# A four-image vision-mixer, attention and expert layer: one TensorE product beside each round of the last attention loop, gathers of the first three images moved into that loop, and 34 of 48 products delta*u moved from the first stage into the loops

## The chip, the cores and the metric

The kernel runs on one core of a Trainium2 chip. The metric is the device time of that core in microseconds (us), the median of three runs.

## The reference

The input is four images of 64 x 64 tokens with 128 channels. Layer 0 adds a scan mixer to them: a group norm, a projection to 256 inner channels and a gate, and then, in three orders of the tokens (forward, backward, sliced), a causal convolution of four taps, SiLU, the projections to delta, B and C, and a selective scan with 16 states; a gate and an output projection follow. Layer 1 adds attention (16 heads of 8, a softmax over all 4096 tokens of an image), a small feed-forward, and last an expert layer in which each of 64 experts picks its 8 best tokens of each image:

```python
def step(h, inp):
    u_, de_, b_, c_ = inp
    dA = jnp.exp(de_[..., None] * A)
    h = h * dA + (de_ * u_)[..., None] * b_[:, None, :]
    y = jnp.einsum('bdn,bn->bd', h, c_)
    return (h, y)
...
delta = jax.nn.softplus(jnp.einsum('dr,brl->bdl', dt_w, dt_raw) + dt_b[None, :, None])
y = selective_scan(x, delta, A, Bm, Cm)
...
logits = jnp.einsum('bsd,ed->bse', x, gate_w) + gate_b
probs = jax.nn.softmax(logits, axis=1)
vals, idx = jax.lax.top_k(probs.transpose(0, 2, 1), K)
...
pooled = jnp.einsum('bked,bke->bed', gathered, topv)
h = jax.nn.gelu(jnp.einsum('ebd,edh->ebh', h, weight1), approximate=False)
out = jnp.einsum('ebh,eho->ebo', h, weight2)
```

Here `de_ * u_` is the product delta*u of the change, and `pooled` is what the gathers make.

## The kernel before

The kernel writes the order of instructions of every engine out by hand: pieces of work are Python generators, each `yield` of which ends a *step*, and a `Pace` (L1350) takes so many steps of a chain of generators whenever its `run` is called. What a step issues goes to the engines' queues in that order, and each engine works through its own queue in order. A generator yields the mark `PE` ahead of a step that issues a TensorE product, and `WAIT` where something that it needs is not made yet. `Bank` (L114) counts PSUM banks: `take` yields `PE`, and again while none is free.

The work is staged as follows (times of the profiled execution).

1. *Fill*, 0 to 2257 us (L1393 to L1399). `Inputs.of_chunk` (L334) makes the scan inputs of 48 chunks (four images, three orders, four chunks of 1024 tokens by 256 channels): convolution L364, SiLU L371, the projections L378 to L400, softplus (L404 to L427, its result `r` is delta). Its end stores delta, multiplies `u` by delta (L431, VectorE) and stores the product as `du` (L432); the stores go by `keep` (L346) to the POOL queue, 1 MB each. Meanwhile `Scans.of_image` (L461) runs the scans of image 0. An image has 384 scan steps; each loads delta and `du` again from memory (SP queue), makes the exponentials (L507, ScalarE), multiplies by B (L514), scans (L523), multiplies by C (L528, all VectorE), and sums over the states on TensorE (L534).
2. *Opening* of image 0, up to 2513 us: queries and values of the attention.
3. *Loops* of images 0 to 2: 2513 to 5066, 5068 to 7657 and 7659 to 10237 us. `Attention.loop` (L850) has 1024 rounds an image. A round of the loop issues four score products (L881, 32 rows of the array each, into two PSUM tiles of a pool of three), two exponentials of 128 x 1024 (L886, ScalarE), and four value products (L895) into an accumulator; it issues the scores of the following round ahead of its own values. After each round `beside(i)` is called. In these loops it runs the next image's scans, `after` of the image before, and the opening of the next one. All of them share one PSUM bank.
4. *Last loop* (image 3), 10240 to 12679 us (L1450 to L1459). Its blocks of 512 tokens are finished one after the other (`by_block`). `beside` is `last.run(0.8)`: four steps in five rounds of one chain, which holds the rest of `after` of image 2, the searches and choices of tokens of images 0 to 2, and `after` of image 3 for the blocks that are finished, all but the last block.
5. *Tail*, 12679 to 12991 us: `after` of the last block, in between the gathers of images 0 to 2 (`gathers.run(3.0)`), the choice of image 3, its gather, and the experts (`answers`, L1282), whose weights are loaded in rooms of 2 MB ahead of use (`prefetch`, L1276), and the scatter.

`Attention.after` (L938) makes for each block: the sums of the softmax loaded, their reciprocals, a store and a load of these, spread out (`shares`, L960); the context times the share (L982, `cT`), the product with `w_comb` (L989, `co`: two banks of two products), a residual and a norm (`first`, L971); cosines of eight columns (L1076, ScalarE); and in `second` (L1002) a transpose (`zT`, L1010), the feed-forward (four `h` products L1023 of 512 columns, then for each of four groups of tokens four `fo` products L1033), a norm, a transpose to `xT` (L1054) and the gate's logits (L1063, `lg`). Each of `co`, `zt`, `fo` and `xT` issues all products of a bank in one step: two, four, four, four. `Experts.search` (L1135) finds the eight best logits of each expert, `choice` (L1156) makes the tokens' weights, and `pool` (L1189), called by `gather` (L1219) once for each 512 tokens, makes `wt` (L1198, four products with a diagonal, one step) and `pool` (L1209, four, one step).

Of the kernel before, what the change touches and what calls it, by code (L numbers as in the profile page):

```python
# [113 lines left out]
class Bank:  # L114


    def __init__(self, pool, n):
        self.pool, self.free = pool, n
# [6 lines left out]
    def take(self, name):  # L125
        yield PE
        while not self.free:
            yield PE
        return self.grab(name)
# [5 lines left out]
def scan_weights(nc, const, load, load_ps, ident, in_proj_w, out_proj_w, dirs):  # L135
# [64 lines left out]
    return w_z, w_out, ws  # L200


class Inputs:
# [130 lines left out]
    def of_chunk(self, b, order, c):  # L334
# [96 lines left out]
        nc.vector.tensor_mul(u, r, u)  # L431
        keep("du", u)  # L432
# [4 lines left out]
class Scans:  # L437
# [23 lines left out]
    def of_image(self, b, made, alone=False):  # L461
# [54 lines left out]
        def step(s):  # L516

            order, c, k, j = steps[s]
            at = 4 * k + j
            dA, dB = tiles.pop(("delta", s)), tiles["du", s]  # L520
            h = self.deep.tile([P, T], F32, tag="h", bufs=2, name=f"h_{b}_{s}")
            first = 0.0 if c == 0 else ends[order, c - 1][:, at : at + 1]
            nc.vector.tensor_tensor_scan(h, dA, dB, first, ALU.mult, ALU.add)  # L523
            if c < NC - 1:
                nc.gpsimd.tensor_copy(ends[order, c][:, at : at + 1], h[:, T - 1 :])  # L525
            if s + 1 < n:
                inputs(s + 1)
            nc.vector.tensor_mul(dB, h, spread[order, c, "C", j % 2])  # L528

# [104 lines left out]
class Attention:  # L634
# [3 lines left out]
    def __init__(self, tc, ctx, w, gate, cols, ident, bank, dram, t1, w_out, sums, sz, x):  # L638
# [64 lines left out]
        self.xn, self.logits, self.angled, self.whole, self.closed = {}, {}, {}, {}, {}  # L703

# [27 lines left out]
    def tokens(self, b, g, angles):  # L732
# [48 lines left out]
        yield  # L781

# [155 lines left out]
    def after(self, b, gs=range(L // QB), to=None):  # L938
# [32 lines left out]
        def first(g):  # L971
# [13 lines left out]
            for half in range(2):  # L985
                ps = yield from self.bank.take(f"co_{b}_{g}_{half}")
                for k in range(2):
                    at = slice((2 * half + k) * P, (2 * half + k + 1) * P)
                    nc.tensor.matmul(ps[:, k * C : (k + 1) * C], cT[:, at], self.w_comb, start=True, stop=True)  # L989
                yield  # L990
                u_h = flat(u[:, 2 * half : 2 * half + 2, :])
                nc.vector.tensor_add(u_h, u_h, ps[:, : 2 * C])
                self.bank.leave()
# [8 lines left out]
        def second(g):  # L1002
# [6 lines left out]
            for k in range(4):  # L1009
                nc.tensor.transpose(ps[:D, k * P : (k + 1) * P], z[:, g * 4 + k, :], self.ident)  # L1010
            yield
# [9 lines left out]
            for f in range(4):  # L1021
                ps = yield from self.bank.take(f"h_{b}_{g}_{f}")
                nc.tensor.matmul(ps, self.w1[:, f * P : (f + 1) * P], zT, start=True, stop=True)  # L1023
# [6 lines left out]
            for k in range(4):  # L1030
                ps = yield from self.bank.take(f"fo_{b}_{g}_{k}")
                for f in range(4):
                    nc.tensor.matmul(  # L1033
                        ps[:, :C], h[:, f, k * P : (k + 1) * P], self.w2[:, f, :], start=(f == 0), stop=(f == 3)
                    )
                yield
# [16 lines left out]
            for k in range(4):  # L1053
                nc.tensor.transpose(ps[:, k * P : (k + 1) * P], u[:, k, :], self.ident)  # L1054
            yield
# [7 lines left out]
            nc.tensor.matmul(ps[rows], self.gate, xT, start=True, stop=True)  # L1063
# [31 lines left out]
class Experts:  # L1095
# [93 lines left out]
    def pool(self, b, g):  # L1189
# [6 lines left out]
        for i in range(4):  # L1196
# [4 lines left out]
            )  # L1201
        yield
# [5 lines left out]
        for i in range(4):  # L1208
            nc.tensor.matmul(ps[:, :E], x[:, i, :], wT[:, i, :], start=(i == 0), stop=(i == 3))  # L1209
        yield  # L1210
# [157 lines left out]
def tile_kernel(tc, ctx, x, in_proj_w, dirs, out_proj_w, attn, gate, weight1, weight2, out):  # L1368
# [45 lines left out]
    block.begin(loop)  # L1414
    with tc.manual_schedule():
# [34 lines left out]
    with tc.manual_schedule():  # L1450
        last = Pace(
            last.parts, experts.biases(),
            *(part for images in pairs[:-1] for part in (experts.search(images, blocks), experts.choice(images, blocks))),
# [3 lines left out]
        block.loop(nb - 1, lambda i: last.run(0.8), True)  # L1457
        last.rest()
    loop.close()  # L1459
    with ExitStack() as end:  # L1460
        block.bank = Bank(end.enter_context(tc.tile_pool(name="end_ps", bufs=7, space=PSUM)), 7)
        with tc.manual_schedule():
            room = experts.room(end, 3)
            gathers = Pace(experts.gather(range(nb - 1)))
            with ExitStack() as pieces:
                block.pieces_of(pieces, 1, opening=False)
                closing = block.after(nb - 1, range(blocks - 1, blocks), experts.rest(pairs[-1], blocks - 1))
                for i, _ in enumerate(closing):
                    if i == 2:
                        experts.prefetch(room, nc.scalar)  # L1470
                    gathers.run(3.0)
            for _ in experts.choice(pairs[-1], blocks - 1):
                gathers.run(3.0)
            gathers.rest()
            experts.prefetch(experts.room(end, 1), nc.scalar)
# [36 lines left out]
```

## Time and profile before

| What | Value |
|---|---|
| Runs | 12969.35, 12983.24, 12982.96 us (median 12982.96) |
| Profiled execution | 12992.53 us, span 12990.6 us |
| Mean TensorE clock granted | 0.958 |
| Fill, opening | 2257 us, 256 us |
| Loops of images 0, 1, 2 | 2553, 2589, 2578 us |
| Last loop | 2438 us |
| Tail | 312 us |

Busy times in the profile: PE is TensorE's products, PEld its weight loads, DVE VectorE, ACT ScalarE, POOL GpSimd, SP the SyncE queue, which only issues transfers. A busy time is a sum over stages of different kinds, so the views by stretch of time, which give the same columns for each stage, are read beside it. The lengths of TensorE's products are modelled; differences between starts are safer. The chain of waits follows the work back from the last instruction, at each step to what released it.

### The profile page before, as it was taken

How to read it: one execution, taken by the hardware profiler on the slowest of the kernel's cores; microseconds unless marked ns; L12 is line 12 of the kernel's file. 1: busy time of each engine (PE TensorE's matmuls, PEld its weight loads, DVE VectorE, ACT ScalarE, POOL GpSimd, SP SyncE). 2: the span in 40 equal slices, each digit the busy share in tenths (PEclk: the TensorE clock that was granted, in tenths of full speed). 3: DMA queues.
4: the chain of work that ended last, by engine and by line, in shares of the span. 5: the costliest groups of instructions: out<-in, count | busy, mean ns of one | idle time of the engine just before them, and what ended most of it. 6: DMA issues, size and time to landing. Idle time of an engine off the chain costs nothing.

```text
span 12990.6 us, 213981 instructions
## 1 busy us (share of the span) xinstructions
PE 12191.8 (94%) x85447; PEld 3937.0 (30%) x85447; DVE 8718.2 (67%) x8674; ACT 10713.3 (82%) x10808; POOL 2930.0 (23%) x3817
## 2 busy tenths in 40 slices
PE   7788888399999999999999999999999999999996
PEld 3333333122222222333322223333222223322225
DVE  6999999788888777888887778888874211121112
ACT  5676766399999988999999889999998888888881
POOL 3323232221212212223232123232321000000000
PEclk9898988699999999999999999999999999999996
DMA  5666776555444455444444445444443100000005
GB/s 157 195 202 195 208 199 190 159 124 122 119 122 111 111 132 134 125 117 111 115 110 110 130 132 126 117 110 116 112 110 97 51 19 11 18 24 11 16 14 183
DMA packets 688512, 1481.86 MB, mean 114 GB/s; under 512 B 187694, under 2 KB 304998, under 8 KB 687254
## 3 DMA queue, kind: packets, MB, share of 16 engines
q1 hardware_dynamic: 499294, 1055.63, 31.8%
q0 software_dynamic: 140192, 302.80, 7.6%
q10 hardware_dynamic: 48024, 109.74, 3.3%
q8 instruction: 669, 10.96, 0.4%
q14 instruction: 333, 2.73, 0.1%
HBM read 1158.77 MB, written 308.81 MB: 113 GB/s over the span
## 4 chain that ended last, share of the span: by engine, by line
PE 81%; DVE 7%; ACT 5%; issue 4%; DMA 3%; SPq 0%; POOL 0%; ACTq 0%; DVEq 0%; POOLq 0%
PE s L881 36%; PE acc L895 30%; PE y L534 4%; PE cv L364 3%; DVE h L523 3%; PE sp L422 2%; PE fo L1033 1%; ACT e L886 1%; PE h L1023 1%; PE xd L378 1%; DVE dB L514 1%; ACT ln L415 0%; DVE du L514 0%; PE out L761 0%; DVE r L427 0%
## 5 line engine op out<-in xcount | busy, mean ns | idle before, releaser
L886 ACT ACTIVATE e<-s 128x1024 f32<-128x1024 f32 x8192 | 7904.8, 1027 | 1053.5 <-PE s L881 882.8
L881 PE MATMUL s<-qm,qT 32*128 32x512 f32 x32768 | 5444.3, 642 | 120.8 <-ACT e L886 61.5
L895 PE MATMUL acc<-e,v 128*32 128x512 f32 x32768 | 4387.5, 607 | 23.8 <-ACT av L904 21.3
L881 PEld LDWEIGHTS s<-qm,qT 32*128 32x128 f32 x32768 | 1801.7, 184 | 3239.3 <-issue 1429.4
L525 POOL COPY ends<-h 128x1 f32<-128x1 f32 x1152 | 1275.0, 1108 | 3352.1 <-DVE h L523 3322.4
L895 PEld LDWEIGHTS acc<-e,v 128*32 128x32 f32 x32768 | 649.0, 108 | 3160.9 <-issue 3021.8
L523 DVE TENSOR_TENSOR_SCAN h<-delta,ends,du 128x1024 f32<-128x1024 f32 x576 | 1350.9, 2345 | 216.2 <-ACT delta L507 185.5
L523 DVE TENSOR_TENSOR_SCAN h<-dA,ends,dB 128x1024 f32<-128x1024 f32 x576 | 1350.6, 2345 | 149.2 <-ACT dA L507 145.8
L514 DVE TENSOR_TENSOR dB<-du,B 128x1024 f32<-128x1024 f32 x768 | 927.9, 1208 | 626.8 <-PE y L534 603.6
L507 ACT ACTIVATE delta<-delta,A 128x1024 f32<-128x1024 f32 x768 | 887.0, 1155 | 153.4 <-PE y L534 142.7
L507 ACT ACTIVATE dA<-delta,A 128x1024 f32<-128x1024 f32 x768 | 888.4, 1157 | 140.9 <-DMA delta<-d_delta 105.4
L528 DVE TENSOR_TENSOR du<-h,C 128x1024 f32<-128x1024 f32 x768 | 935.3, 1218 | 0.1
L528 DVE TENSOR_TENSOR dB<-h,C 128x1024 f32<-128x1024 f32 x768 | 935.0, 1217 | 0.0
L514 DVE TENSOR_TENSOR du<-du,B 128x1024 f32<-128x1024 f32 x768 | 920.9, 1199 | 0.0
L364 PE MATMUL cv<-xn,conv 128*128 128x512 f32 x1024 | 499.9, 642 | 25.7 <-DVE xn L299 17.3
L563 POOL DMA_DIRECT2D d_y<-o x512 | 327.6, 668 | 781.9 <-DVE o L550 720.3
L910 POOL DMA_DIRECT2D d_ctx<-av x512 | 263.4, 523 | 1055.8 <-ACT av L904 1046.5
L534 PE MATMUL y<-du,sel 128*32 128x256 f32 x6144 | 488.2, 391 | 13.1 <-DVE du L528 13.1
L534 PE MATMUL y<-dB,sel 128*32 128x256 f32 x6144 | 491.7, 393 | 3.4 <-DVE dB L528 3.4
L523 DVE TENSOR_TENSOR_SCAN h<-delta,du 128x1024 f32<-128x1024 f32 x192 | 438.4, 2283 | 52.0 <-ACT delta L507 45.5
L523 DVE TENSOR_TENSOR_SCAN h<-dA,dB 128x1024 f32<-128x1024 f32 x192 | 438.4, 2283 | 40.0 <-ACT dA L507 38.4
L1026 DVE TENSOR_SCALAR h<-h,b 128x512 f32<-128x512 f32 x124 | 92.7, 748 | 514.0 <-PE s L881 514.0
(256 smaller groups left out, 7648.6 us busy)
## 6 DMA issues: line engine op xcount, KB each, us to landing
delta<-d_delta SPq DMA_DIRECT2D x768, 512.0 KB
du<-d_du SPq DMA_DIRECT2D x576, 512.0 KB
du<-d_du ACTq DMA_DIRECT2D x192, 512.0 KB
d_u<-u POOLq DMA_DIRECT2D x48, 1024.0 KB, 5.8
B<-d_bc SPq DMA_DIRECT2D x96, 512.0 KB
C<-d_bc SPq DMA_DIRECT2D x96, 512.0 KB
d_delta<-r POOLq DMA_DIRECT2D x48, 1024.0 KB, 5.1
d_du<-u POOLq DMA_DIRECT2D x48, 1024.0 KB, 6.9
```

The costliest lines, as they stand in the source:

```text
L364: nc.tensor.matmul(ps[:, cut], w["conv"][:, k, m * P : (m + 1) * P], reads(k, g), start=(k == 0), stop=(k == 3))
L507: nc.scalar.activation(tiles["delta", s], t, AF.Exp, scale=A)
L514: nc.vector.tensor_mul(tiles["du", s], du, spread[order, c, "B", j % 2])
L523: nc.vector.tensor_tensor_scan(h, dA, dB, first, ALU.mult, ALU.add)
L525: nc.gpsimd.tensor_copy(ends[order, c][:, at : at + 1], h[:, T - 1 :])
L528: nc.vector.tensor_mul(dB, h, spread[order, c, "C", j % 2])
L534: nc.tensor.matmul(y[32 * g : 32 * g + 32, : T // 4], self.sel[:, j // 2, :], hC[:, 256 * g : 256 * g + 256], start=(j == 0), stop=(j == 3),)
L563: nc.gpsimd.dma_start(out=to.rearrange("p (i j) -> p i j", i=SLICES)[:, :, at : at + n], in_=rows.rearrange("p (i j) -> p i j", i=SLICES),)
L881: nc.tensor.matmul(s_ps[:, k, :], qT[at : at + 32, kc * P : (kc + 1) * P], queries[j, qb][at : at + 32, :], start=True, stop=True,)
L886: nc.scalar.activation(e, s_ps, AF.Exp, scale=1.0 / math.sqrt(D))
L895: nc.tensor.matmul(accs[j, qb][32 * k : 32 * k + 32, :], v[:, kc, h * VW : h * VW + 32], es[i][k // 2][:, k % 2, :], start=(kc == 0), stop ...
L910: nc.gpsimd.dma_start(out=self.context[b][h * D : h * D + D, cut], in_=av[32 * k : 32 * k + D, :])
```

## The change

- `Bank` gets a flag `patient`. While it is set and no bank is free, `take` yields `WAIT` and not `PE`.
- `early` names 14 chunks, the twelve of image 0 and two of image 1, that keep the product delta*u in the fill. For the other 34, `Scans.product(s)` makes it at the end of scan steps in loops 0 to 2 (not in the fill): eight pieces of 128 x 256 a chunk, for the chunk that comes next. In one step it loads 128 KB each of delta and u on the SP queue, two steps later it multiplies them (VectorE) and stores 128 KB to `d_du` on the POOL queue; the tiles have one buffer each. That is 272 pieces in all.
- `between` yields `PE` between the products of a bank while `fine` is set, which it is in the last loop only: `co`, `zt`, `fo` and `xT` then issue one product a step; `wt` and `pool` issue two.
- `h` and `lg`, one product of 512 columns each before, are two of 256 columns everywhere, in two steps in the last loop.
- The last loop's `beside` takes up to three steps of the chain that do not begin with a product, and then at most one that does.
- The gathers of images 0 to 2 stand in that chain, each behind its choice. In the tail, only image 3 is gathered, and the fourth room of weights is asked for ahead of the choice.

```diff
--- before.py
+++ after.py
@@ -115,7 +115,7 @@
 
 
     def __init__(self, pool, n):
-        self.pool, self.free = pool, n
+        self.pool, self.free, self.patient = pool, n, False
 
     def grab(self, name):
         assert self.free
@@ -125,6 +125,8 @@
     def take(self, name):
         yield PE
         while not self.free:
+            while self.patient and not self.free:
+                yield WAIT
             yield PE
         return self.grab(name)
 
@@ -200,6 +202,11 @@
     return w_z, w_out, ws
 
 
+def early(b, order, c):
+
+    return b == 0 or (b == 1 and order == 0 and c < 2)
+
+
 class Inputs:
 
 
@@ -428,8 +435,9 @@
             self.leave()
         self.middle = False
         keep("delta", r)
-        nc.vector.tensor_mul(u, r, u)
-        keep("du", u)
+        if early(b, order, c):
+            nc.vector.tensor_mul(u, r, u)
+            keep("du", u)
         self.made[b, order, c] = made
         yield
 
@@ -526,6 +534,27 @@
             if s + 1 < n:
                 inputs(s + 1)
             nc.vector.tensor_mul(dB, h, spread[order, c, "C", j % 2])
+            if not alone:
+                product(s)
+
+        def product(s):
+
+            order, c, k, j = steps[s]
+            part, turn = divmod(4 * k + j - 8, 3)
+            chunk = (b, order, c + 1) if c + 1 < NC else (b, order + 1, 0) if order < 2 else (b + 1, 0, 0)
+            if part < 0 or turn == 1 or chunk not in made or early(*chunk):
+                return
+            of, m, at = made[chunk], part // 4, part % 4 * (T // 4)
+            cut = slice(m * P, (m + 1) * P), slice(at, at + T // 4)
+            if turn == 0:
+                for name in ("delta", "u"):
+                    t = self.extra.tile([P, T // 4], F32, tag=f"x_{name}", name=f"x_{name}_{b}_{s}")
+                    nc.sync.dma_start(out=t, in_=of[name][cut])
+                    tiles["x", name] = t
+            else:
+                t, u = tiles.pop(("x", "delta")), tiles.pop(("x", "u"))
+                nc.vector.tensor_mul(t, t, u)
+                nc.gpsimd.dma_start(out=of["du"][cut], in_=t)
 
         def total(s, y):
             order, c, k, j = steps[s]
@@ -701,6 +730,7 @@
         self.small = ctx.enter_context(tc.tile_pool(name="a_small", bufs=2))
         self.u, self.q, self.v, self.context, self.total, self.t2 = {}, {}, {}, {}, {}, {}
         self.xn, self.logits, self.angled, self.whole, self.closed = {}, {}, {}, {}, {}
+        self.fine = False
 
     def begin(self, loop):
 
@@ -779,6 +809,11 @@
         turned(nc, a, turns.rearrange("p h d -> p (h d)"))
         self.angled[b] += 1
         yield
+
+    def between(self, k, n=4):
+
+        if self.fine and k + 1 < n:
+            yield PE
 
     def norm(self, out, src, name):
 
@@ -987,6 +1022,7 @@
                 for k in range(2):
                     at = slice((2 * half + k) * P, (2 * half + k + 1) * P)
                     nc.tensor.matmul(ps[:, k * C : (k + 1) * C], cT[:, at], self.w_comb, start=True, stop=True)
+                    yield from self.between(k, 2)
                 yield
                 u_h = flat(u[:, 2 * half : 2 * half + 2, :])
                 nc.vector.tensor_add(u_h, u_h, ps[:, : 2 * C])
@@ -1008,6 +1044,7 @@
             ps = yield from self.bank.take(f"zt_{b}_{g}")
             for k in range(4):
                 nc.tensor.transpose(ps[:D, k * P : (k + 1) * P], z[:, g * 4 + k, :], self.ident)
+                yield from self.between(k)
             yield
             zT = self.piece([D, 512], "p0", name=f"zT_{b}_{g}")
             nc.vector.tensor_scalar_mul(zT, ps[:D], self.cos_ry[:, 2:3])
@@ -1020,7 +1057,10 @@
             h = self.one.tile([P, 4, 512], F32, tag="h", bufs=max(1, self.n - 1), name=f"h_{b}_{g}")
             for f in range(4):
                 ps = yield from self.bank.take(f"h_{b}_{g}_{f}")
-                nc.tensor.matmul(ps, self.w1[:, f * P : (f + 1) * P], zT, start=True, stop=True)
+                for k in range(2):
+                    at = slice(k * 256, k * 256 + 256)
+                    nc.tensor.matmul(ps[:, at], self.w1[:, f * P : (f + 1) * P], zT[:, at], start=True, stop=True)
+                    yield from self.between(k, 2)
                 yield
                 if self.n == 2:
                     nc.vector.tensor_scalar(h[:, f, :], ps, self.b1[:, f : f + 1], 0.0, ALU.add, ALU.max)
@@ -1033,6 +1073,7 @@
                     nc.tensor.matmul(
                         ps[:, :C], h[:, f, k * P : (k + 1) * P], self.w2[:, f, :], start=(f == 0), stop=(f == 3)
                     )
+                    yield from self.between(f)
                 yield
                 nc.vector.tensor_add(u[:, k, :], u[:, k, :], ps[:, :C])
                 self.bank.leave()
@@ -1052,6 +1093,7 @@
             ps = yield from self.bank.take(f"xT_{b}_{g}")
             for k in range(4):
                 nc.tensor.transpose(ps[:, k * P : (k + 1) * P], u[:, k, :], self.ident)
+                yield from self.between(k)
             yield
             xT = self.piece([P, 512], "p0", name=f"xT_{b}_{g}")
             nc.vector.tensor_copy(xT, ps)
@@ -1060,7 +1102,10 @@
             yield
             ps = yield from self.bank.take(f"lg_{b}_{g}")
             rows = slice(E, 2 * E) if to else slice(0, E)
-            nc.tensor.matmul(ps[rows], self.gate, xT, start=True, stop=True)
+            for k in range(2):
+                at = slice(k * 256, k * 256 + 256)
+                nc.tensor.matmul(ps[rows, at], self.gate, xT[:, at], start=True, stop=True)
+                yield from self.between(k, 2)
             yield
             if to:
                 for t in to:
@@ -1199,6 +1244,7 @@
                 ps[:, i * E : (i + 1) * E], self.chosen[b // 2][rows, at : at + P], self.diagonal[rows, b // 2, :],
                 start=True, stop=True,
             )
+            yield from self.block.between(i, 3 if i == 1 else 0)
         yield
         wT = self.some.tile([P, 4, E], F32, tag="wT", name=f"wT_{b}_{g}")
         nc.vector.tensor_copy(wT.rearrange("p i e -> p (i e)"), ps[:, : 4 * E])
@@ -1207,6 +1253,7 @@
         ps = yield from bank.take(f"pool_{b}_{g}")
         for i in range(4):
             nc.tensor.matmul(ps[:, :E], x[:, i, :], wT[:, i, :], start=(i == 0), stop=(i == 3))
+            yield from self.block.between(i, 3 if i == 1 else 0)
         yield
         into = self.pooled[:, :, b]
         if g == 0:
@@ -1412,6 +1459,7 @@
     block.bank = bank
     loop = ExitStack()
     block.begin(loop)
+    scans.extra = loop.enter_context(tc.tile_pool(name="s_extra", bufs=1))
     with tc.manual_schedule():
         last = Pace()
         n = 3 * NC * NB
@@ -1450,29 +1498,40 @@
     with tc.manual_schedule():
         last = Pace(
             last.parts, experts.biases(),
-            *(part for images in pairs[:-1] for part in (experts.search(images, blocks), experts.choice(images, blocks))),
+            *(
+                part for images in pairs[:-1]
+                for part in (experts.search(images, blocks), experts.choice(images, blocks), experts.gather(images))
+            ),
             block.after(nb - 1, range(0, 4)), block.after(nb - 1, range(4, 6)), block.after(nb - 1, range(6, blocks - 1)),
             experts.search(pairs[-1], blocks - 1),
         )
-        block.loop(nb - 1, lambda i: last.run(0.8), True)
+        block.fine = bank.patient = True
+
+        def beside(i):
+
+            for _ in range(3):
+                if last.then is not PE:
+                    last.run(1.0)
+            if last.then is PE:
+                last.run(1.0)
+
+        block.loop(nb - 1, beside, True)
         last.rest()
+        block.fine = False
     loop.close()
     with ExitStack() as end:
         block.bank = Bank(end.enter_context(tc.tile_pool(name="end_ps", bufs=7, space=PSUM)), 7)
         with tc.manual_schedule():
             room = experts.room(end, 3)
-            gathers = Pace(experts.gather(range(nb - 1)))
             with ExitStack() as pieces:
                 block.pieces_of(pieces, 1, opening=False)
                 closing = block.after(nb - 1, range(blocks - 1, blocks), experts.rest(pairs[-1], blocks - 1))
                 for i, _ in enumerate(closing):
                     if i == 2:
                         experts.prefetch(room, nc.scalar)
-                    gathers.run(3.0)
+            experts.prefetch(experts.room(end, 1), nc.scalar)
             for _ in experts.choice(pairs[-1], blocks - 1):
-                gathers.run(3.0)
-            gathers.rest()
-            experts.prefetch(experts.room(end, 1), nc.scalar)
+                pass
             for _ in experts.gather(pairs[-1]):
                 pass
             for _ in experts.answers(end, out):
```

## The prediction, on record before the changed kernel ran

> **What bounds the kernel now.** I read the page first, then the fill, the loops and the tail each by themselves, because the page is an average over stages with different limits. On the page, TensorE is busy for 94% of the span and owns the chain that ended last. Its two attention lines (the scores of L881 and the values of L895) hold two thirds of that chain.
>
> ```profile
> PE 12191.8 (94%) x85447; PEld 3937.0 (30%) x85447; DVE 8718.2 (67%) x8674; ACT 10713.3 (82%) x10808; POOL 2930.0 (23%) x3817
> ...
> PE 81%; DVE 7%; ACT 5%; issue 4%; DMA 3%; SPq 0%; POOL 0%; ACTq 0%; DVEq 0%; POOLq 0%
> ```
>
> The busy times by stage (columns: stretch, length, then PE, PEld, DVE, ACT and POOL busy, PE clock, DMA share, GB/s) tell the stages apart: the fill, the first loop, the last loop, the tail.
>
> ```profile
> 0.00:2257.00 2257.00, 1875.71 (x6821) 755.29 (x6821) 2033.90 (x1543) 1526.08 (x1223) 730.28 (x909) 0.89 0.67 193
> 2513.00:5066.00 2553.00, 2538.18 (x19802) 733.75 (x19798) 2064.74 (x1673) 2387.75 (x2498) 591.44 (x809) 1.00 0.49 120
> 10240.00:12678.00 2438.00, 2415.54 (x17248) 708.98 (x17244) 368.36 (x947) 2016.18 (x2109) 178.81 (x313) 0.99 0.07 20
> 12678.00:12990.00 312.00, 214.80 (x1538) 170.63 (x1534) 89.15 (x201) 31.85 (x51) 26.05 (x47) 0.63 0.56 190
> ```
>
> The fill is nearest to VectorE (90%), both loops are TensorE's, and the tail is a chain of dependent steps with TensorE at 0.63 of its clock. The fill's groups give the product that the change moves 110 us of VectorE:
>
> ```profile
> L431 DVE TENSOR_TENSOR u<-r,u 128x2048 f32<-128x2048 f32 x48 | 110.0, 2292 | 1.7
> ```
>
> But the chain of waits in the fill alternates: for long stretches it runs between TensorE and ScalarE, and VectorE's work lies beside it (start, length, line).
>
> ```profile
> 1045.16 10.52 PE cv L364 x24
> ...
> 1055.70 1.12 ACT u L371
> ...
> 1056.87 2.84 PE xd L378 x6
> ```
>
> In the last loop I timed rounds by what stands beside them. In the timeline (start, length, line; lengths are modelled, so I take differences of starts):
>
> ```profile
> 10704.85 1.14 PE L881 MATMUL s<-qm,qT 32*128 32x512 f32 x8
> 10705.92 1.07 PE L895 MATMUL acc<-e,v 128*32 128x512 f32 x8
> 10706.92 1.37 PE L881 MATMUL s<-qm,qT 32*128 32x512 f32 x8
> 10708.22 1.07 PE L895 MATMUL acc<-e,v 128*32 128x512 f32 x8
> ...
> 11007.08 1.16 PE L1033 MATMUL fo<-w,h 128*128 128x128 f32 x8
> 11008.17 1.14 PE L881 MATMUL s<-qm,qT 32*128 32x512 f32 x8
> ...
> 11495.01 0.71 PE L989 MATMUL co<-w_comb,cT 128*128 128x128 f32 x4
> 11495.65 1.14 PE L881 MATMUL s<-qm,qT 32*128 32x512 f32 x8
> ```
>
> An empty round takes 2.07 us (10704.85 to 10706.92) or 2.30 (the next; its second scores wait 0.23 for the exponentials, there being three buffers), alternating. A burst of four fo products (eight passes) costs 1.09, two co products (four passes) 0.64. Of the co burst 0.21 pass before its second pass and 0.20 between its last pass and the next scores; the middle passes cost 0.11. So a product alone (two passes) costs about 0.21 + 0.20 = 0.42, against 0.27 as a quarter of the fo burst. In the tail, the gathers of images 0 to 2 stand between the closing's products, and the answers (L1240) start behind the last gather (chain of waits: start, length, line):
>
> ```profile
> 12751.49 2.00 PE fo L1033 x8
> 12753.49 1.60 PE pool L1209 x8
> 12755.09 1.90 PE wt L1198 x8
> 12756.99 2.00 PE fo L1033 x8
> ...
> 12857.62 1.97 PE pool L1209 x8
> 12859.99 1.97 PE h L1240 x8
> ```
>
> [...] 0.20 is lost where a 128-row product gives way to 32-row scores, and the co at 10265.21 held the attention for 2.2 us while its input came. [...] in the start of the last loop the reciprocal's store leaves at 10258.50 and the load behind it at 10260.85, landing at 10264.4.
>
> **Part 1, the fill.** 34 of 48 products leave: 34 x 2.29 = 78 us of VectorE and 34 stores on POOL. Following the chain over 0 to 2257, 17 of the 48 lie on it; of the moved ones that is 12 to 14. Where a product leaves that is not on the chain, the next wait (the convolution, L364, then ScalarE's L371 to L415) is just as late. Value: 13 x 2.29 = **-30**. Bounds: -10 (only the stretches where VectorE alone makes the chain) and -78 (all).
>
> **Part 2, loops 0 to 2.** 272 pieces: each two SP loads, one VectorE product of 0.42 and one POOL store; 272 x 0.42 = 114 us of VectorE over 7,740 us of loops. Loop 0 has 488 us of VectorE idle, and TensorE needs of the scans only their totals, one step later. The cover is that idle time; without it the whole 114 would count. A new load waits on SP for the previous piece's store to land (one buffer); behind it wait the scan's delta and du loads, and for these the exponentials. A step takes 2557/384 = 6.7 us and the page's 1 MB stores land in 5 to 7, so that a piece of an eighth is there within the step between: no wait. The h and lg products come in halves in these loops too, about 2 us a loop. Value **+12**, bounds 0 and +50.
>
> **Part 3, last loop, work.** The order of instructions shows 196 rounds with products before and 667 after. Before: fo 60 x 1.09, h 60 x 0.60, co 30 x 0.64, zt and xT 15 x 0.585 each, lg 15 x 1.00 = 153 us. After: fo 240 x 0.42, h halves 120 x 0.30 [...], co 60 x 0.42, zt and xT 60 x 0.26 each, lg halves 30 x 0.55 = 209.5: **+56.5**. The gathers of 24 groups give 48 wt and 48 pool rounds of four passes, unseen in a loop; a co burst has as many: 96 x 0.64 = **+61**. A round with 0.23 or more beside it takes away its neighbour's wait for the exponentials. If all 1024 rounds alternated, that wait would be 512 x 0.23 = 118. Before, products take away 16. After, 667/2 x 0.23 = 77, of which about 20 returns in 170 empty rounds that stand alone: **-41**. Work: +77.
>
> **Part 4, last loop, new waits.** The three-steps rule and the patient bank bring each product as early as its chain allows, and TensorE keeps program order: where its input isn't there, attention stops, and the exponentials behind it too. Worked out per place from the durations of before: the start (cT at 10264.5, co now at round 3, 10247.8) 17; the first gather after either choice 11 each (two searches of 4.4, the copy, a POOL step); the first co of the first blocks 6 and of block 6 12; four cosines with a table load 2.5 each; norm chain to xT 0.9 times seven and 7.6 once; the two-buffer ring of the sums' loads (a period of 14.9 us against 12.1 in five rounds) 18. Together 100. Before, rounds longer than their kind add to 38. **+62**; bounds -38 (none waits) and +110.
>
> **Part 5, tail.** The closing no longer has gathers between its products: the second co comes 4.5 earlier, zt 6, h and fo 19 (39.7 becomes 20.3), xT to the choice 12, and after the choice 8 gathers instead of 11.5 remain, 3.5 x 4.38 = 15. **-57**; what is late next is the answers' weights, now asked for before the choice. Bounds -40 and -65.
>
> **Sum.** -30 + 12 + 77 + 62 - 57 = +64. The profiled execution took 12992.53 (span 12990.6), 9.6 above the median of the three runs; against it the sum gives 13,056, against the median 13,047. I take 13,047.
>
> **Rivals.** *No wait in the last loop* (the faster one): three VectorE or ScalarE steps a round are enough lead for each product, and even the 38 of before vanish. Then -30 + 12 + 77 - 38 - 57 = -36: 12,947. It decides where the waits of all products in the last loop total under about 10. For it speaks that VectorE is only 15% busy there; against it, that the chains hold two or three dependent transfers of 3 to 6 us, which no step count shortens. *The fill gives all its 78*: 64 - 48 = +16, 12,999; VectorE's 90% speaks for it, the alternating chain against it. *A lone product pays no switch* (0.27, as in a burst): 64 - 56 = +8, 12,991; the 0.20 before the scores speaks against it. *SP held up by the pieces*: +38 more, 13,085; the whole step between store and load speaks against it. *The products do not come one beside a round*: the order of instructions excludes it.
>
> **Chances.** About 0.2% (26 us) is what a measurement of this kernel can tell from no change. Likeliest case 0.47 (own range 13,010 to 13,085), SP 0.05: slower 0.52. All of the fill 0.10 and no switch 0.10: same 0.20. No waits 0.18, and two of the three mild cases together 0.10 (12,940 and below): faster 0.28. The range from 12,930 to 13,100 leaves out the last of these and the ends of the bounds above.
>
> **What would show it.** The fill's end at about 2227 instead of 2257, with VectorE's L431 14 times. Loops 0 to 2 each within 15 us of before. The last loop at 2,560 to 2,590 instead of 2,438, with fo rounds of 2.49 and TensorE waiting 60 us or more for cT, z, xT and the choice's output by the waits view. From the loop's end to the answers' first product 125 us instead of 181. I am wrong if the last loop stays under 2,500: then the single products hide where I let them pay; or if the fill ends 60 or more earlier.

## The result, and the profile after

The changed kernel took 13054.98 us (median of four runs, 13046.53 to 13055.76), the kernel before 12976.15 (four runs, 12967.25 to 12983.24). The ratio is 1.0058, with a 95% interval of 1.0043 to 1.0074: slower by 0.6%. The profiled execution took 13046.53, its span 13044.4, that is 53.8 more than the span of before; the medians differ by 78.8. The profiled execution of before lay 16 above its median of four runs, that of the changed kernel 8 below its own, so a stage of one trace can be off by some us.

By stage, from the two traces (cut at the last store of delta, at the starts of the exponentials, at the copy of the last accumulator, and at the answers' first product):

| Stage | Before | After | Difference | Predicted |
|---|---|---|---|---|
| Fill, to the last store of delta | 2253.8 | 2223.2 | -30.6 | -30 |
| Opening | 259.4 | 259.7 | +0.3 | |
| Loops of images 0, 1, 2 | 2554.8, 2591.0, 2581.4 | 2554.2, 2603.4, 2582.2 | +12.6 | +12 |
| Last loop | 2439.4 | 2577.3 | +137.9 | +139 |
| Tail up to the answers | 180.3 | 118.3 | -62.0 | -57 |
| Answers and scatter | 130.6 | 126.0 | -4.6 | |

On the page, TensorE's busy time is about what it was (12191.8 before), although the span grew; its share of the chain fell from 81% to 78%, and transfers gained a point:

```profile
PE 12178.7 (93%) x85767; PEld 3924.0 (30%) x85767; DVE 8731.2 (67%) x8912; ACT 10713.8 (82%) x10808; POOL 3116.2 (24%) x4055
...
PE 78%; DVE 7%; ACT 5%; DMA 4%; issue 3%; SPq 1%; POOL 1%; ACTq 0%; DVEq 0%; POOLq 0%
```

The page mixes the tail, which lost gathers, with the last loop, which got them. The busy times by stage (the same four stages and columns as before) take them apart:

```profile
0.00:2257.00 2257.00, 1870.43 (x6867) 754.01 (x6867) 1976.25 (x1533) 1528.26 (x1227) 729.88 (x887) 0.89 0.64 180
2483.00:5034.00 2551.00, 2536.18 (x19792) 731.08 (x19788) 2093.55 (x1768) 2386.47 (x2498) 660.32 (x905) 1.00 0.53 135
10222.00:12799.00 2577.00, 2503.21 (x17788) 763.68 (x17780) 385.13 (x995) 2018.85 (x2109) 177.67 (x314) 0.98 0.07 21
12799.00:13044.00 245.00, 122.17 (x1162) 90.66 (x1160) 73.81 (x153) 31.21 (x51) 26.05 (x47) 0.67 0.63 216
```

In the last loop TensorE is busy for 86 us more than before (2503.2 against 2417.2 over 10240 to 12680), and idle for 51 more. The list of TensorE's waits in that loop (engine, line, what it waited for: us in total, times, longest) adds up to 73.5; its longest rows are:

```profile
PE co L1024 <- DVE cT L1017: 24.2, 4, 17.5
PE co L1024 <- DVE x L1028: 14.3, 12, 2.3
PE wt L1243 <- DVE chosen L1231: 10.5, 2, 5.6
PE s L916 <- ACT e L921: 7.6, 8, 1.3
PE xT L1095 <- DVE x1r L830: 6.7, 1, 6.7
```

Before, the list adds up to 22.4:

```profile
PE s L881 <- ACT e L886: 12.8, 6, 5.4
...
PE co L989 <- DVE cT L982: 2.2, 1, 2.2
```

The first row of the changed kernel's list is mostly one event, at the loop's start. The chain of waits shows the reciprocal's store and the load behind it, for which cT waits; the timeline of TensorE shows the product behind cT and what the wait leaves behind.

```profile
10241.08 2.31 DMA d_share<-sum
...
10243.41 3.63 DMA part<-d_share
```

```profile
10247.89 0.80 PE L1024 MATMUL co<-w_comb,cT 128*128 128x128 f32 x2 [17.53 <-DVE cT L1017]
10248.61 2.09 PE L916 MATMUL s<-qm,qT 32*128 32x512 f32 x8
10250.63 1.79 PE L930 MATMUL acc<-e,v 128*32 128x512 f32 x8
10252.35 0.49 PE L1024 MATMUL co<-w_comb,cT 128*128 128x128 f32 x2
```

TensorE stands for 17.53 us, and the scores and values behind it then take 2.02 and 1.72 us from start to start, against 1.07 and 1.00 in a round that follows no wait. The clock granted over these scores and values (10248.60 to 10252.35) was 0.53, and 1.00 over 10252.80 to 10258.00; the prediction had noted a low clock in the tail only (0.63). Behind the waits for both choices (4.92 and 5.58 us) the scores take 2.02 as well. A single fo product costs what was worked out, 0.42 (10643.44 to 10643.86). The lines also show where the wait for the exponentials stands: the scores of 10641.15, with no product ahead of them, are followed by their values after 1.30 us in place of 1.07, while those of 10643.86, behind a product, are followed after 1.07.

```profile
10641.15 1.37 PE L916 MATMUL s<-qm,qT 32*128 32x512 f32 x8
10642.45 1.06 PE L930 MATMUL acc<-e,v 128*32 128x512 f32 x8
10643.44 0.49 PE L1073 MATMUL fo<-w,h 128*128 128x128 f32 x2
10643.86 1.14 PE L916 MATMUL s<-qm,qT 32*128 32x512 f32 x8
```

To divide the 138 us, I took 1022 rounds of each last loop, from the start of one round's values to the start of the next one's. With no product and no wait such a round takes 2.067: 0.996 to the next scores, and 1.071 from these to their values. What it takes beyond that is put down as follows. A round with a product is charged what its kind takes where TensorE does not stand (the tenth percentile of the kind). In a round without one, up to 0.26 between scores and values is a wait for the exponentials. The rest, in both, is called stops: waits of TensorE and the rounds that they slow.

| us in 1022 rounds | Before | After | Difference | Predicted |
|---|---|---|---|---|
| Products of `after` (co, zt, h, fo, xT, lg) | 166.9 | 220.0 | +53.1 | +56 |
| Gathers (wt, pool) | 0 | 56.3 | +56.3 | +61 |
| Waits for exponentials | 112.9 | 69.4 | -43.5 | -41 |
| Stops | 42.0 | 114.0 | +72.0 | +62 |

One product costs: fo 0.42 (a burst of four 1.09), co 0.42 (a burst of two 0.64), half an h 0.41 (a whole one 0.84), half an lg 0.58 (a whole one 1.00), half a wt or pool 0.58 to 0.59. Of the rounds without a product, 297 of 355 wait for the exponentials, before 478 of 826.

### The profile page after: what moved, and what is told of

Same layout as the page of the kernel before. It is cut to its first block, busy times and chain, and to the rows that moved or that the text cites. A ratio compares the mean times of both kernels' runs of the same rounds, so it can differ in the third digit from the quotient of the medians.

```text
span 13044.4 us, 216243 instructions
## 1 busy us (share of the span) xinstructions
PE 12178.7 (93%) x85767; PEld 3924.0 (30%) x85767; DVE 8731.2 (67%) x8912; ACT 10713.8 (82%) x10808; POOL 3116.2 (24%) x4055
## 4 chain that ended last, share of the span: by engine, by line
PE 78%; DVE 7%; ACT 5%; DMA 4%; issue 3%; SPq 1%; POOL 1%; ACTq 0%; DVEq 0%; POOLq 0%
PE s L916 34%; PE acc L930 28%; PE y L563 4%; PE cv L371 3%; DVE h L531 3%; PE sp L429 2%; PE fo L1073 1%; ACT e L921 1%; PE xd L385 1%; PE h L1062 1%; DVE dB L522 1%; DMA du<-d_du 1%; DMA part<-d_share 0%; ACT ln L422 0%; ACT e L417 0%
## 5 line engine op out<-in xcount | busy, mean ns | idle before, releaser
L916 PE MATMUL s<-qm,qT 32*128 32x512 f32 x32768 | 5375.5, 643 | 109.1 <-DMA qT<-d_q 58.6
L916 PEld LDWEIGHTS s<-qm,qT 32*128 32x128 f32 x32768 | 1769.1, 184 | 2824.9 <-PE s L916 1290.4
L533 POOL COPY ends<-h 128x1 f32<-128x1 f32 x1152 | 1333.6, 1159 | 2900.5 <-DVE h L531 2895.7
L1078 DVE TENSOR_TENSOR x1r<-x1r,fo 128x128 f32<-128x128 f32 x128 | 36.6, 286 | 744.3 <-PE fo L1073 744.3
L531 DVE TENSOR_TENSOR_SCAN h<-delta,du 128x1024 f32<-128x1024 f32 x192 | 438.8, 2285 | 53.8 <-ACT delta L515 44.8
```

What stands on the lines that cost most here:

```text
L916: nc.tensor.matmul(s_ps[:, k, :], qT[at : at + 32, kc * P : (kc + 1) * P], queries[j, qb][at : at + 32, :], start=True, stop=True,)
```

## The experiments

Each ratio is to the kernel before on the same chip; its medians in these sets lay at 12980 to 12984. "Base" of a last loop is the time of its 1022 rounds less the stops, counted as in the last table: 2392 before, 2458 in the changed kernel.

**du_only.** The kernel before with the move of delta*u alone.

```diff
+        if early(b, order, c):
+            nc.vector.tensor_mul(u, r, u)
+            keep("du", u)
...
+            if not alone:
+                product(s)
```

> The kernel before with the move of delta*u alone (34 of 48 products out of the fill into loops 0 to 2; h and lg stay whole, the last loop and the tail are those of before). Theory (the pieces ride in VectorE's idle time, the chain of the fill had about 13 of the moved products on it): fill -30, loops 0 to 2 +10, so about 12,956, 20 under before. Rival 1 (the 12.8 us by which loops 0 to 2 grew is from the halved h and lg products, not from the pieces): loops +0, about 12,946. Rival 2 (the fill's gain is lost later, at the opening): no change, 12,976.

Measured: 12967.07, ratio 0.9991 (0.9985 to 0.9998), 13 under before. The fill lost 24.4, loops 0 to 2 grew by 0, 11.5 and 6.0, the last loop was 5.4 shorter. So the fill's gain is kept, and the loops grow without the halves of h and lg: rivals 1 and 2 fall, and 13 of the theory's 20 came. Loop 1 is 5 to 16 longer in every trace with the pieces, and 2 in the run without them that follows. The growth of loop 2 is not firm: it goes from -2 to +6 over the traces, and this profiled execution was 12 above its median.

**last_only.** The changed kernel with all products left in the fill.

```diff
-    return b == 0 or (b == 1 and order == 0 and c < 2)
+    return True
```

> The changed kernel with all 48 products left in the fill: the last loop and the tail of the change alone, with h and lg in halves. Theory (the parts add): last loop +137, tail -62 and -5 in the answers, halves in loops 0 to 2 about +3, fill 0: about 13,050, 74 over before. Rival (the parts interact, since moved loads and stores change what the last loop finds): under 13,030 or over 13,070.

Measured: 13062.39, ratio 1.0062 (1.0049 to 1.0075). Last loop 2576.9, tail 118.0, fill 2252.1, loops 0 to 2 together 0.2 longer than before: the halves of h and lg cost nothing there. The parts add within some 10 us; the time is between the theory's and the rival's bound, and the stages are the theory's.

**bursts.** No splitting in the last loop.

```diff
-        block.fine = bank.patient = True
+        bank.patient = True
```

> The changed kernel with the splitting off: in the last loop a bank's products go in one step again (co two, zt, fo, xT four, h and lg two halves, wt and pool four), all else as changed, gathers in the loop. Theory (a lone product pays the switch to and from the scores, 0.15 us more than as a quarter of a burst): -56 for the dense products, -25 for the gathers, +41 for the waits for exponentials that come back: last loop about 2,537, in all about 13,015. Rival (the waits for inputs are what costs; splitting is nearly free): within 10 of 13,055. Rival 2 (bursts wait as often and longer): over 13,055.

Measured: 13068.4, ratio 1.0068 (1.0054 to 1.0081): not 40 faster than the change. My theory falls. By the ratios it is 9 slower, within the intervals, so that the time does not part the two rivals; its last loop, 2590.2, is 13 longer. Products beside rounds cost 217 us in place of 276, 59 less, and 40 of waits for exponentials are back (110 for 69), so that the base is 19 shorter, 2439. But the stops grew by 32, to 146: bursts wait longer, as the second rival had it. A burst meets the same unfinished input, as the timeline of that kernel's first blocks shows:

```profile
10281.45 1.22 PE L1024 MATMUL co<-w_comb,cT 128*128 128x128 f32 x4 [4.42 <-DVE x L1028]
10282.60 2.09 PE L916 MATMUL s<-qm,qT 32*128 32x512 f32 x8
10284.62 1.94 PE L930 MATMUL acc<-e,v 128*32 128x512 f32 x8
```

The co waits 4.42 for the residual of the bank before it, since VectorE works in order and stands at the next group's cT, whose share is still being loaded (eight such waits, 41.4 us, in the first 175 us of that loop); and in the round behind it the scores take 2.02 from start to start, and the values 1.94.

**const_inputs.** The products beside a round read a constant weight tile, as said in its expectation, so their results no longer depend on what is made for them (one of eight lines shown).

```diff
+    def fed(self, made, fixed):
+        return fixed if self.fine else made
...
-                    nc.tensor.matmul(ps[:, k * C : (k + 1) * C], cT[:, at], self.w_comb, start=True, stop=True)
+                    nc.tensor.matmul(ps[:, k * C : (k + 1) * C], self.fed(cT[:, at], self.w2[:, 2 * half + k, :]), self.w_comb, start=True, stop=True)
```

> The changed kernel in which the last loop's products beside a round (co, zt, h, fo, xT, lg, wt, pool) read a constant weight tile instead of what VectorE, ScalarE and the transfers make for them; these still do all their work, and the single bank is still waited for. The outputs lose that dependence. Theory (the waits for inputs cost 47 us by the waits view, and some 10 more in slow-clock rounds behind the longest): last loop about 2,520, in all about 13,000. Rival (the waits only stand in for others, of the bank or the exponentials): less than 20 off, over 13,035.

Measured: 13019.92, ratio 1.0029 (1.0019 to 1.0040). The last loop took 2542.5, 35 less, between theory and rival, and its stops are 79 for 114. The wait at the start changed its name rather than going: the first co is free, but the next needs the bank, and the residual that empties it stands, in VectorE's order, behind a cT that waits for its load (in the changed kernel such waits hold VectorE for 85.8 us of the last loop). From the list of TensorE's waits in that kernel:

```profile
PE co L1028 <- DVE x L1032: 30.2, 14, 15.3
```

So an unready input holds TensorE by two ways, the product's own and the single bank behind VectorE's order.

**lead.** A due product goes out first in its round.

```diff
+            if last.then is PE:
+                last.run(1.0)
             for _ in range(3):
                 if last.then is not PE:
                     last.run(1.0)
-            if last.then is PE:
-                last.run(1.0)
```

> The changed kernel with one reordering in the last loop's helper: a product that is due goes out first in a round, and the up to three other steps follow it, so that no product is queued in the round in which its input was queued; the same products, one a round. Theory (most short waits come from products queued directly behind their input; the long ones, at the start and behind the choices, hang on transfers and searches and stay): waits of TensorE 73 to about 45, last loop about 2,550, in all about 13,028. Rival (a round is too short to help): over 13,045.

Measured: 13061.54, ratio 1.0065 (1.0050 to 1.0080). The theory falls, and its rival holds: last loop 2582.1. TensorE's wait for cT fell to 18.6 and for the choice to 6.1, but that for exponentials rose from 7.6 to 22.6. The list of ScalarE's waits says why (0.5 for the first row in the changed kernel, and no second row):

```profile
ACT z L1127 <- DVE z L111: 8.8, 4, 2.8
ACT top L1213 <- DVE low L1211: 4.1, 2, 2.1
```

With this order the cosines and the choice's exponentials reach ScalarE before their inputs, and the attention's exponentials stand behind them. One round of lead moves waits of this length to another queue.

**spaced.** The order of lead, and rounds let pass behind each slow step: those of the diff, and likewise 2 or 3 ahead of or behind cT's load, the cosines, the norm ahead of xT, the searches and the choices.

```diff
+    def aged(self, n):
+        until = self.round + n
+        while self.fine and self.round < until:
+            yield WAIT
...
             nc.sync.dma_start(out=t, in_=rows(self.total[b][blocks]))
             yield
+            yield from self.aged(4)
             nc.vector.reciprocal(t, t)
             nc.gpsimd.dma_start(out=rows(share), in_=t)
             yield
+            yield from self.aged(3)
```

> The reordering of the run before, and besides a number of rounds (1 to 5) that the chain of the last loop lets pass behind each transfer, search, cosine and norm before it queues what needs it. The work is the same. Theory (waits and the slow-clock rounds behind them are 78 of the 137 us by which the last loop grew): nearly all go, last loop about 2,495, in all about 12,975. Rival (the rest of the growth, not the waits, carries it; or spreading the work makes other waits): over 13,020.

Measured: 12982.39, ratio 1.0002 (0.9993 to 1.0011), no different from before, and 73 under the changed kernel's median. Last loop 2509.0: the base is 2455, as in the changed kernel (2458), and the stops fell from 114 to 49. The products are the same; only the stops went. The longest row left in the list of TensorE's waits:

```profile
PE co L1033 <- DVE cT L1026: 14.5, 11, 1.5
```

**whole_bursts.** bursts, with h and lg in one product of 512 columns.

```diff
-                for k in range(2):
-                    at = slice(k * 256, k * 256 + 256)
-                    nc.tensor.matmul(ps[:, at], self.w1[:, f * P : (f + 1) * P], zT[:, at], start=True, stop=True)
-                    yield from self.between(k, 2)
+                nc.tensor.matmul(ps, self.w1[:, f * P : (f + 1) * P], zT, start=True, stop=True)
```

> The run with the splitting off, and h and lg whole again as well (512 columns in one product), so that every product of the last loop has the form that it has in the kernel before; helper, patience and gathers as changed. Theory (a halved h costs 0.4 us more than a whole one; otherwise splitting costs in products what it saves in waits for exponentials): 60 x 0.4 = 25 under the 13,068 of that run, about 13,043, no better than the changed kernel by more than 15. Rival (bursts are cheaper than single products, as the prediction's 56 us had it): under 13,010.

Measured: 13060.7, ratio 1.0064 (1.0049 to 1.0079). The base is 2438, the stops are 147. With the kernel before's own form of every product the loop is no shorter than with single ones. The 25 us that I expected of whole h products did not appear: a whole h costs 0.84, two halves in a burst the same, and two single halves 0.83.

**spaced_bursts.** The edits of whole_bursts and spaced together.

> Both at once: products in bursts with whole h and lg, and the reordering and spacing of the run spaced; delta*u moved and gathers in the loop as changed. Theory (the waits are what made the last loop dear, and bursts of whole products are 15 to 40 cheaper than single ones): about 12,950, under the kernel before. Rival (waits return, as a burst needs the bank longer): over 12,990.

Measured: 13001.4, ratio 1.0016 (1.0009 to 1.0023): 59 under whole_bursts, 19 over spaced, and over the 12,990 of the rival, which holds. The base is 2434, 21 under that of spaced, but the stops are 87 for 49, among them h products that wait for the bank (10.6 us in four waits). Spacing is worth about as much with bursts (63 in the last loop) as with single products (68), and with the spacing the single ones are the faster: splitting is not the cause of the loss.

**du_two.** du_only with two buffers for the tile that holds delta and then the product.

```diff
-                    t = self.extra.tile([P, T // 4], F32, tag=f"x_{name}", name=f"x_{name}_{b}_{s}")
+                    t = self.extra.tile([P, T // 4], F32, tag=f"x_{name}", bufs=2 if name == "delta" else 1, name=f"x_{name}_{b}_{s}")
```

> The kernel before with the move of delta*u alone, as in the first experiment, but with two buffers for the tile that holds delta and then the product, so that a load need not wait on SP for the store of the piece before. Theory (those waits, 763 us of SP in the second loop by the waits view, cost nothing, as SP stood at its scan buffers as long before; the growth of loops 1 and 2 is VectorE's): within 5 of 12,967. Rival (SP's wait delays the scans' loads): loops 1 and 2 lose 10 or more, under 12,957.

Measured: 12964.95, ratio 0.9987 (0.9980 to 0.9993), 2 from du_only. The lists of waits on SP's queue in the loop of image 1 show what SP waits for ahead of a piece's loads, first in du_only (the store of the piece before), then in du_two (its product, since the tile of u still has one buffer):

```profile
SPq L550 <- DMA d_du<-x_delta: 762.9, 83, 23.6
```

```profile
SPq L550 <- DVE x_delta L554: 425.1, 76, 20.5
```

Of the wait for the store 21.7 us are left, but it was replaced: all of SP's waits in that loop sum to some 2090 us in both runs, and to 2140 before, when SP waited 1593 us there for the scans' totals. So SP has this time to spare. In the traces loops 1 and 2 are 3 and 8 shorter than in du_only, about as the rival asked; the times do not bear it out (2 us, within the intervals), and du_only's profiled execution was 12 above its median.

**spaced_tail.** spaced, with the gathers of images 0 to 2 in the tail.

```diff
-                for part in (experts.search(images, blocks), experts.choice(images, blocks), experts.gather(images))
+                for part in (experts.search(images, blocks), experts.choice(images, blocks))
...
+            gathers = Pace(experts.gather(range(nb - 1)))
```

> The run spaced with the gathers of images 0 to 2 back in the tail as before. Theory (with the waits gone the gathers cost 74 us of products in the loop less some 10 of saved waits for exponentials, and save 66 behind it: even): loop about 2,445, tail and answers 66 longer, in all about 12,984, within 10 of spaced. Rival (moving them is a gain of its own): over 13,000.

Measured: 12996.97, ratio 1.0010 (1.0002 to 1.0019), 15 over spaced. The last loop is 50.6 shorter (2458.4) and the tail 64.0 longer (181.8). By both, moving the gathers into a loop with few stops gains some 13. That lies past the bound of 10 that I gave the theory and 3 short of the 13,000 that the rival needed: neither is settled, and the gain is small.

**paced.** The version meant to beat both: before's last loop, whole bursts at an even pace, with the gathers behind both choices; delta*u moved; the tail of the change.

```diff
+            *(experts.gather(images) for images in pairs[:-1]),
...
-        block.loop(nb - 1, lambda i: last.run(0.8), True)
+        block.loop(nb - 1, lambda i: last.run(1.0), True)
```

> A version meant to beat both: the kernel before with the move of delta*u (two buffers as in du_two), its last loop with whole bursts and even pace, raised from 0.8 to 1.0 step a round, and the gathers of images 0 to 2 in that loop behind both choices, where the chain has steps to spare; the tail as changed, without them. Theory: 48 rounds of eight passes at 1.26 less 5 of saved waits = +55 in the loop, -62 in the tail, -4 in the answers: about 11 under the 12,967 of the first experiment, 12,956. Rival (the raised pace brings the waits of the changed kernel back): over 12,980.

Measured: 12956.11, ratio 0.9977 (0.9967 to 0.9986), faster than both. Last loop 2488.3 (+52 on du_two's 2436.4), tail 118.9 (-61). TensorE's waits in the last loop come to 30, little over the 22 of before:

```profile
PE s L908 <- ACT e L913: 17.6, 5, 10.5
PE co L1016 <- DVE cT L1009: 6.9, 1, 6.9
```

## Why the prediction was right

The time forecast was 13,047, the measured median 13,055. The forecast of +64 lies between the 53.8 by which the traces differ and the 78.8 by which the medians do. Each stage lies within 5 us of its forecast, and so do three of the last loop's four terms; inside the terms there is some luck.

*The fill* (-30) came as read from the chain: -30.6 in the changed kernel, -24 and -29 in the runs with the move alone. The other 47 of the 78 us taken off VectorE (14 products left, 32.1 us, for 48 and 110.0) did not shorten it, as forecast for what lies beside TensorE's and ScalarE's chain: that chain holds 5 of the 14 products left, where it held 17 of 48. The rival that the fill gives all its 78 falls.

*Loops 0 to 2* (+12) grew by 12.6, in the runs with the move alone by 17 and 7. The halves, to which I gave 6, cost nothing. One step was wrong: "no wait" for the new loads. In loop 1 SP stands 764 us for the stores in 83 waits, 9 us each; but all its waits there sum to no more than before, so this took from time that SP had to spare, and the rival of 38 more for it falls. Why loop 1 grows and loop 0 does not stays open; VectorE's pieces take 40 us in loop 1 (96 of 0.42, which is what L992, of that size, took in the kernel before).

*The last loop's work* (+77) was +66, and each term came near: +53 for +56, +56 for +61, -43 for -41. A lone fo or co costs 0.42, as worked out, so that the rival "a lone product pays no switch" falls. The 0.20 ahead of the scores shows that time is lost there; its cause is not shown. An h was priced too low: I took 0.60, which is what a whole one adds to a round of 2.30 that already waits, and 0.30 for a half, an estimate with no switch in it; they cost 0.84 and 0.41, a half as much as a lone fo. Sixty of the one before and 120 of the other after are some 14 us each, and cancel in the difference: that is luck. A half gather costs 0.58 to 0.59, not 0.64. The statement that splitting costs 56 us was true of the products and not of the loop, since most of it comes back in saved waits: with bursts the base is 19 or 20 shorter, and the stops are longer by more.

*The new waits* (+62) measured +72, in part by luck. The places were right, and their sizes mixed: 17.5 at the start (17 forecast), 10.5 behind the choices (22), 6.7 in three more waits for cT (18), 6.7 behind the lone block's norm (7.6) and 3.7 behind the other norms (6.3), 2.5 for cosines (10), 14.3 in the ring of the first blocks (18). These come to 62 where I had 100. What made up for it I had not counted: the rounds slowed behind a wait, and a few waits for exponentials. TensorE is idle for 51 us more; the other 21 of the 72, an estimate by subtraction, are a slower TensorE (granted clock 0.50 to 0.53 in the rounds behind the start and the choices). What these stops are worth is shown by spaced, which keeps every product, loses 68 in the last loop and comes out even with the kernel before: without them the products' +66 would have been paid for by the fill and the tail. The mechanism is the helper: three steps a round queue a product directly behind the transfer or search that feeds it. The even pace of before left time between them.

*The tail* (-57) measured -62, and the answers gained 5 more. The answers start at the last gather, as before:

```profile
12916.04 1.97 PE pool L1255 x8
...
12918.40 1.97 PE h L1287 x8
```

Of the rivals, "no wait in the last loop" had the waits right in sign: taking most of them away brought 73, to 12,982 and not to 12,947, as 49 us of stops remain.

## What to carry to other kernels

An engine that works in order should get a dependent step no earlier than its input is due: filling every slot as soon as the program order allows turned 42 us of stops into 114, and spacing the same steps out took back 65. Cost a product in a loop with its neighbours: a lone fo costs 0.42, against 0.27 as a quarter of a burst, but can also remove a wait of 0.23: here +53 for the products stood against -43 of waits. Work moved out of a tail into a busy loop is worth only the difference of its price there, here 64 against 51; a wait that goes away under one name can stand under another, so the sum of an engine's waits is read beside the row that changed; and a move that bundles a gain of 13 (delta*u) with a loss should be split and timed by parts.

## What the runs showed of the hardware that was not expected

TensorE's long waits had an aftermath. Behind 17.5 us of idling the next round took 4.16 us (10248.61 to 10252.77, scores to scores) where a round with a co takes 2.49, and the clock granted to its scores and values was 0.53; behind the choices' waits of 4.92 and 5.58 the next wt rounds took 4.69 and 4.93, against a median of 2.88. From 11576 to 11582, behind the second of them, the granted clock was 0.50. Even the 4.42 us wait in bursts was followed by a round of some 4 us of products. In all four the scores took 2.02 us, for 1.07 in a round that follows no wait. In this loop, where TensorE is busy for 2503 of 2577 us, some 21 of the 72 us that the stops grew by are a slower TensorE and not idling (an estimate: 72 less the 51 of added idle time).
